# Four small reorderings in an eight-layer transformer kernel on one core: a new order of TensorE's work in the last attention, adapter coefficients moved forward, transposes of the identity at the start, weight sums placed first

## Chip, cores and metric

The kernel runs on one core of a Trainium2 chip. The metric is the time of one execution on the device in microseconds (us). The engines of the core are named as in the profile: PE is TensorE's matmul side and PEld its weight load, DVE is VectorE, ACT is ScalarE, POOL is GpSimd, SP is SyncE, whose queue issues nearly all DMAs. A trailing q (PEq, SPq, DVEq) means the engine's sequencer.

## What is computed

The input is x of shape (2, 512, 512): two batches of 512 tokens of width 512, all in fp32. Eight layers follow each other, each with a layer normalisation in front and the input added to its output. Cut to what matters:

```python
x = x + attn_latent(_layernorm(x))   # 32 heads, keys of 4 latent values, no mask
x = x + ffn_lora(_layernorm(x))      # one matrix plus a rank-16 adapter chosen per batch
x = x + attn_gqa(_layernorm(x))      # 32 query heads in 8 groups of 4, head size 128, rotary, causal
x = x + ffn_lora(_layernorm(x))
x = x + attn_mla(_layernorm(x))      # latent keys and values, causal
x = x + ffn_moe(_layernorm(x))       # top 2 of 8 adapters per token
x = x + attn_mha(_layernorm(x))      # 32 heads of size 16, rotary, causal
x = x + ffn_moe(_layernorm(x))
```

The last attention computes, for each head,

```python
scores = jnp.einsum('bqhd,bkhd->bhqk', q, k) * scale
scores = scores + (1.0 - causal) * MASK_VAL
probs = jax.nn.softmax(scores, axis=-1)
ctx = jnp.einsum('bhqk,bkhd->bqhd', probs, v).reshape(b, s, e)
```

In the adapter layer, `lora_start_indices` say from which batch on which adapter is used. The kernel turns them into one factor per row of the stacked adapter matrices (0 or 1).

## The kernel before

**Memory.** x stays in SBUF as eight tiles of 128 tokens. `xT[b]` is the normalised input of a batch, transposed, in four pieces of 128 channels. PSUM has eight banks of 128 x 512 fp32; `turn()` hands them out in a fixed cycle of eight, so an instruction that takes a bank waits until whatever read the bank eight turns earlier is done. The bank's names in the profile (`sc`, `pj`, `tp`, `av`) say only which of the eight it is.

**Order.** Tile, the layer below the kernel, schedules VectorE, ScalarE, GpSimd and SP by itself, close to the order of the program; each engine then runs its instructions strictly in that order. In the attentions TensorE's order is written out by hand (`manual_schedule`).

**The start.** `Block.__init__` issues the first four loads of x and makes the identity on GpSimd. `attn_latent_small` (first attention) issues its weights and the other four tiles of x on SP, then many small loads. `prepare(0)` normalises the first four tiles (statistics and `xn` on VectorE, one power on GpSimd at L197), transposes each on TensorE (L182), copies it with ScalarE (L187), and multiplies with the latent weights (L156): the first chain gives the keys (L415), the second `cq` (L420), from which the heads follow.

**Adapter layers.** `ffn_lora` runs twice. At its first call (L622 to L638) it loads the start indices and a constant table and computes the factor `k.coef` in eight small VectorE instructions, then scales the adapter matrix `la` with it (L639), multiplies adapters on TensorE (L646, eight outputs), adds the base matrix on VectorE (L650), and multiplies the tokens (L156 chains). The second call finds `k.coef` made.

**Grouped attention.** `attn_gqa` computes the queries of two heads at a time with a Strassen-like scheme: seven half-size products instead of eight, for which `token_sums` (VectorE, L768) and `weight_sums` (GpSimd, L781 to L784, four instructions per pair of heads) prepare sums. The rotary step of a query is two half-height products with the sine on VectorE (L829, L830), then on GpSimd the product with the cosine (L831) and the sum (L832). Scores (L229) need the result. At the start the order written down is latents, keys, token sums, the first pair's weight sums, its queries, the second pair's weight sums, values.

**Last attention.** For each batch, 32 heads are done in eight quartets of four heads. The four heads of a quartet sit in four groups of 32 partitions, so their products can run side by side in the array. A quartet takes on TensorE:
- 16 `score` products S (L1460), one for each of four query tiles and four heads, 128, 256, 384 or 512 columns wide because of the causal mask. VectorE adds the mask and takes the maximum of each row (L1470, and a second instruction that reads the result).
- `maxima`, M: four transposes of these maxima (L1484), then VectorE adds them to the queries (`qm`, L1486), so that the next products come out with the maximum already subtracted.
- 16 `transposed` products T (L1496), keys by queries, 512, 384, 256 or 128 columns wide; ScalarE takes the exponential of each (L1506). After the fourth of a key tile GpSimd masks its diagonal (L1510).
- `values`, V: 64 products with the values into one bank (L1521), copied by ScalarE (L1529).
- `divide`, D: four transposes of the sums (L1535), reciprocal and multiplication on VectorE (L1538, L1539).

`run_quartets` interleaves, at step u, the scores of quartet u+1 with the transposed products of quartet u, one to one; the first four scores and the first four transposed products stand in two blocks. After the first block of each step comes D of quartet u-1; at the end of the step V of quartet u, and then M of quartet u+1. The program has two versions of this attention under a branch, causal by leaving out and causal by adding a mask; the first ran in the profile.

Of the kernel before, what the change touches and what calls it, by code (L numbers as in the profile page):

```python
# [31 lines left out]
F32 = mybir.dt.float32  # L32
I32 = mybir.dt.int32
AF = mybir.ActivationFunctionType
ALU = mybir.AluOpType
AX = mybir.AxisListType

B, S, D = 2, 512, 512
P = 128
NT = S // P  # L40
# [5 lines left out]
class Block:  # L46


    def __init__(self, ctx, tc, x, out):
        nc = self.nc = tc.nc  # L50
        self.tc = tc
        self.out = out
        pool = lambda name, bufs, **kw: ctx.enter_context(tc.tile_pool(name=name, bufs=bufs, **kw))
        self.const = pool("const", 1)
        self.w = pool("w", 2)
        self.work = pool("work", 2)
        self.small = pool("small", 6)
        self.psum = pool("psum", 2, space=bass.MemoryType.PSUM)
        self.turns = 0
        self.held = None  # L60
        self.coef = None

        self.x = [
            self.const.tile([P, D], F32, tag=f"x{t}", name=f"x{t}") for t in range(NTILES)
        ]
        self.source = x
        self.load_x(0)


        self.room = self.const.tile([P, 4 * KC * S], F32, tag="room", name="room")  # L70
        parts = self.room.rearrange("p (n c s) -> p n c s", n=4, c=KC)
        self.xT = [parts[:, b] for b in range(B)]
        self.spare = [parts[:, 2 + i] for i in range(2)]
        self.spare_turn = 0
        self.ident = self.const.tile([P, P], F32, tag="ident", name="ident")
        make_identity(nc, self.ident)
        self.mhalf = self.const.tile([P, 1], F32, tag="mhalf", name="mhalf")
        nc.gpsimd.memset(self.mhalf, -0.5)
        self.ones = self.const.tile([P, 1], F32, tag="ones", name="ones")
        nc.gpsimd.memset(self.ones, 1.0)  # L80

    def load_x(self, b):
        for t in range(b * NT, b * NT + NT):
# [245 lines left out]
    def run_quartets(n, score, maxima, transposed, values, after, extra=()):  # L329
# [5 lines left out]
        for u in range(-1, n + 1):  # L335
# [24 lines left out]
            if u + 1 < n:  # L360
                maxima(u + 1)


def attn_latent_small(k, a):

# [6 lines left out]
    nc, tc = k.nc, k.tc  # L372
    with ExitStack() as ctx:
        lp = ctx.enter_context(tc.tile_pool(name="a", bufs=2))
# [18 lines left out]
        for i in range(2):  # L393
            m = one([P, NT, P], f"nm{i}")
# [81 lines left out]
        for piece in prepare(0):  # L476
            piece()
        k.masks()
        extra = prepare(1) + [fold, fold_bias]

        quartets = [(b, half, i) for b in range(B) for half in range(2) for i in range(4)]
# [123 lines left out]
            k.run_quartets(len(quartets), score, maxima, transposed, values, after, extra)  # L605


def ffn_lora(k, a):

    nc, tc = k.nc, k.tc
    R = 48
    with ExitStack() as ctx:
        lp = ctx.enter_context(tc.tile_pool(name="f0", bufs=2))
        w = k.load(a["f0_w"], [P, KC, D], "w8", 5)

        la = k.load(a["f0_a"], [P, D], "w3", 6)
        lb = k.load(a["f0_b"], [P, D], "w3", 6)  # L620
        bias = k.load_row(a["f0_bias"], D, "bias")
        if k.coef is None:  # L622
            k.coef = k.const.tile([P, 1], F32, tag="coef", name="coef")
            starts = k.load_row(a["f0_starts"], 4, "f0_starts", dtype=I32)
            rows = k.load(a["c_lora"], [P, 4], "c_lora", 1)
            startf = lp.tile([P, 4], F32, tag="startf", name="startf")
            nc.vector.tensor_copy(startf, starts)


            c = lp.tile([P, 4], F32, tag="le", name="le")  # L630
            nc.vector.tensor_scalar(c, startf, rows[:, 3:4], None, ALU.is_le)
            r = lp.tile([P, 3], F32, tag="rank", name="rank")
            both = lp.tile([P, 2], F32, tag="both", name="both")
            nc.vector.tensor_tensor(both, c[:, 1:3], c[:, 2:4], ALU.mult)
            nc.vector.tensor_tensor(r[:, 0:2], c[:, 1:3], both, ALU.subtract)
            nc.vector.tensor_copy(r[:, 2:3], both[:, 1:2])
            nc.vector.tensor_tensor(r, r, rows[:, 0:3], ALU.mult)
            nc.vector.tensor_reduce(k.coef, r, AX.X, ALU.add)  # L638
        nc.vector.tensor_scalar(la, la, k.coef, None, ALU.mult)  # L639

        adapted = [k.w.tile([P, KC, D], F32, tag="w8", name="adapted", bufs=5) for b in range(B)]
        for m in range(KC):
            out = [k.turn() for b in range(B)]
            for b in range(B):
                own = slice(64 * b, 64 * b + R)
                nc.tensor.matmul(  # L646
                    out[b], la[own, bass.ts(m, P)], lb[own], start=True, stop=True
                )
            for b in range(B):
                nc.vector.tensor_tensor(adapted[b][:, m], out[b], w[:, m], ALU.add)  # L650

        for t in range(NT):
            k.add_bias(t, bias)
        for b in range(B):
            for t in range(NT):
                ps = k.turn()
                k.chain(
                    ps, [(k.xT[b][:, c, bass.ts(t, P)], adapted[b][:, c]) for c in range(KC)]
                )
                k.add_to_x(b * NT + t, ps)  # L660
                if b == 0:
                    k.layernorm(NT + t, k.turn, bias=bias)
                else:
                    k.layernorm(t, k.turn, back=True)


def attn_gqa(k, a, bound):
# [7 lines left out]
    nc, tc = k.nc, k.tc  # L675
    G, J = 8, 4
    with ExitStack() as ctx:
# [3 lines left out]
        tables = {}  # L681
# [20 lines left out]
        def latents(b, m):  # L702
            if m == 0:
                ckvT[b] = one([P, KC, S], "ckvT")
            ps = k.turn()
            k.chain(ps, [(wdk[:, c, bass.ts(m, P)], k.xT[b][:, c]) for c in range(KC)])
            nc.scalar.copy(ckvT[b][:, m], ps)
# [85 lines left out]
        def queries(m, i, part):  # L793

            b = groups[m][1]
            a11, a12, diff, a22, both, less, last = ws[m, i]
            x = lambda c, n: tokens(b, c, n)
            add = lambda out, ps, sb: nc.vector.tensor_tensor(out, ps, sb, ALU.add)  # L798
            copies = ends[0][:, :S]
            if part == 0:  # L800
                ps = k.turn()
                product(ps[:, first], a11, x(0, 0))
                product(ps[:, second], both, xs[0])
                nc.scalar.copy(copies, ps)
            elif part == 1:
                q0, q1 = qs[m, 2 * i], qs[m, 2 * i + 1] = [
                    lp.tile([P, S], F32, tag="q", name="q", bufs=3) for r in range(2)
                ]
                ps = k.turn()
                product(ps[:, first], less, xs[1])  # L810
                product(ps[:, second], diff, xs[2])
                add(q0[:, second], ps[:, first], copies[:, first])
                add(q1[:, first], ps[:, second], q0[:, second])
                for out, of in ((q0[:, second], q0[:, second]), (q1[:, second], q1[:, first])):
                    nc.gpsimd.tensor_tensor(out, of, copies[:, second], ALU.add)
            else:
                pair = q0, q1 = qs[m, 2 * i], qs[m, 2 * i + 1]
                ps = k.turn()
                product(ps[:, first], a12, x(1, 0))
                product(ps[:, second], a22, xs[3])  # L820
                add(q0[:, first], ps[:, first], copies[:, first])
                add(q1[:, first], ps[:, second], q1[:, first])
                ps = k.turn()
                product(ps[:, first], last, x(1, 1))
                add(q0[:, second], ps[:, first], q0[:, second])
                for q in pair:
                    t2 = k.work.tile([P, S], F32, tag="xn", name="t2")
                    sin = tables["sinq"]
                    nc.vector.tensor_tensor(t2[0:64], q[64:128], sin[64:128], ALU.mult)  # L829
                    nc.vector.tensor_tensor(t2[64:128], q[0:64], sin[0:64], ALU.mult)  # L830
                    nc.gpsimd.tensor_tensor(q, q, tables["cosq"], ALU.mult)  # L831
                    nc.gpsimd.tensor_tensor(q, q, t2, ALU.add)  # L832

        def softmax(m, j):
# [67 lines left out]
                wdk = k.load(a["b_wdk"], [P, KC, D], "w8", 5)  # L902

        with tc.manual_schedule(engines={mybir.EngineType.PE}):
            for m in range(KC):
                latents(0, m)
            prepare_keys(0)
            token_sums(0)
            weight_sums(0, 0)
            for part in range(3):  # L910
                queries(0, 0, part)
            weight_sums(0, 1)
            prepare_values(0)
            probs = {}
            for n in range(len(units) + J + 1):
# [448 lines left out]
def attn_mha(k, a, exact, rooms):  # L1364
# [9 lines left out]
    with ExitStack() as ctx:  # L1374
# [64 lines left out]
        def core(b, causal):  # L1439
# [104 lines left out]
                )  # L1544

            with tc.manual_schedule(engines={mybir.EngineType.PE}):
                k.run_quartets(8, score, maxima, transposed, values, [divide])
            ctxT = k.other()
            for c in range(T):
                tp = k.turn()  # L1550
# [195 lines left out]
```

## Time and profile before

| what | us |
|---|---|
| runs shown | 2143.32, 2146.19, 2143.63 (median 2143.63) |
| the profiled execution's own time | 2145.26 |
| span of its profile | 2143.50 |
| last attention, batch 0, first score to last transposed sums | 1805.6 to 1906 |
| the same, batch 1 | 1964.8 to 2066 |

The span is the time from the first to the last instruction of the profiled execution; 1.76 us of its own time lie outside. Positions in the profile are counted from the span's start. In a line of the order of time, the columns are start, duration, engine, line and operation, outputs and inputs with their tile names, the shape, the count of merged instructions, and in brackets how long the engine had been idle in front and what ended that. In a stretch's line of busy times, each engine has its busy time and count, then the clock granted to TensorE (1.00 is full), the share of the DMA engines and GB/s.

An fp32 product shows as two passes of one instruction each. Ends of matmuls are modelled, so a matmul's duration says less than the distance between two starts.

### The profile page before, as it was taken

The page shows a single profiled execution, that of the slowest core. Times are in us where ns is not written, and L with a number is a line of the kernel's source. Part 1 is how long each engine was busy: PE and PEld are TensorE (multiplying, and loading weights), DVE is VectorE, ACT ScalarE, POOL GpSimd, SP SyncE. Part 2 cuts the span into 40 slices and gives each one's busy share as a digit, 9 for nine tenths or more (in the row PEclk, how much of TensorE's full clock was granted, in tenths as well). Part 3 has the DMA queues.
Part 4 walks back from the last instruction along what each step waited for, and adds up shares of the span by engine and source line. Part 5 has one row for each costly group of instructions (what it writes and reads, how often), then busy time and mean ns, then how long its engine had stood idle before and what let it go on. Part 6 is the DMA issues. An engine that isn't in the chain of part 4 may idle for free. (4 is left out here: it accounts for less than half of the span.)

```text
span 2143.5 us, 40021 instructions
## 1 busy us (share of the span) xinstructions
PE 2048.5 (96%) x15500; PEld 1147.2 (54%) x15500; DVE 1349.5 (63%) x3571; ACT 749.0 (35%) x2072; POOL 972.9 (45%) x1243
## 2 busy tenths in 40 slices
PE   6999989899999999999999989999999989999988
PEld 3444435566666666666665444545454544554554
DVE  6578754665575566666765557666666675745745
ACT  2455631222232222222222145454445212532531
POOL 1101023767665557666762256555555544215220
PEclk9999999899999999999999999999999999999999
DMA  2000022222222222222221321010101002002001
GB/s 98 16 1 1 20 89 73 86 70 70 89 70 74 71 83 77 73 89 70 72 75 31 115 60 53 21 53 21 49 22 51 2 30 45 1 2 40 2 2 40
DMA packets 70221, 107.44 MB, mean 50 GB/s; under 512 B 13698, under 2 KB 50690, under 8 KB 63236
## 3 DMA queue, kind: packets, MB, share of 16 engines
q1 hardware_dynamic: 69380, 103.71, 15.7%
q8 instruction: 126, 2.06, 0.4%
q10 hardware_dynamic: 640, 1.05, 0.3%
q14 instruction: 75, 0.61, 0.1%
HBM read 80.61 MB, written 2.10 MB: 39 GB/s over the span
## 5 line engine op out<-in xcount | busy, mean ns | idle before, releaser
L250 ACT ACTIVATE room<-room,nmax 128x128 f32<-128x128 f32 (+3 forms) x384 | 212.1, 554 | 478.5 <-DVE nmax L240 477.4
L261 POOL TENSOR_SCALAR room<-room,invs 128x128 f32<-128x128 f32 (+3 forms) x384 | 197.5, 534 | 144.9 <-DVE invs L258 144.9
L301 PE MATMUL sc<-turned,vals 32*128 32x128 f32 (+7 forms) x1090 | 188.4, 424 | 0.0
L301 PE MATMUL tp<-turned,vals 32*128 32x384 f32 (+7 forms) x720 | 164.4, 412 | 2.1 <-DVE q L798 2.1
L229 PE MATMUL sc<-kT,q 128*32 128x256 f32 (+3 forms) x1496 | 135.8, 398 | 11.4 <-DVE invs L258 7.9
L274 DVE STREAM_TRANSPOSE turned<-room 128x1152 f32<-128x1152 f32 x80 | 109.0, 1363 | 42.8 <-POOL room L261 39.8
L301 PEld LDWEIGHTS sc<-turned,vals 32*128 32x128 f32 (+1 forms) x1090 | 122.5, 171 | 9.2 <-issue 4.4
L301 PE MATMUL pj<-turned,vals 32*128 32x256 f32 (+7 forms) x602 | 126.1, 424 | 1.3 <-DVE turned L274 1.3
L831 POOL TENSOR_TENSOR q<-q,cosq 128x512 f32<-128x512 f32 x64 | 95.4, 1491 | 60.0 <-DVE t L830 60.0
L197 POOL TENSOR_TENSOR rstd<-ve,mhalf 128x1 f32<-128x1 f32 x80 | 44.3, 557 | 168.5 <-DVE ve L195 141.3
L229 PE MATMUL tp<-kT,q 128*32 128x32 f32 (+15 forms) x1072 | 98.6, 401 | 11.2 <-DVE invs L258 7.1
L301 PEld LDWEIGHTS tp<-turned,vals 32*128 32x128 f32 (+1 forms) x720 | 97.0, 168 | 14.6 <-issue 6.9
L229 PE MATMUL pj<-kT,q 128*32 128x96 f32 (+15 forms) x1048 | 100.5, 417 | 2.9 <-POOL q L1096 1.9
L156 PE MATMUL sc<-w,room 128*128 128x512 f32 (+1 forms) x224 | 100.5, 595 | 0.0
L301 PE MATMUL av<-turned,vals 32*128 32x384 f32 (+7 forms) x372 | 99.9, 419 | 0.0
L156 PE MATMUL sc<-w,ctxT 128*128 128x512 f32 x208 | 94.2, 595 | 0.0
L250 ACT ACTIVATE probs<-probs,nmax 128x128 f32<-128x128 f32 (+3 forms) x128 | 71.1, 556 | 65.6 <-DVE nmax L240 64.3
L261 POOL TENSOR_SCALAR probs<-probs,invs 128x128 f32<-128x128 f32 (+3 forms) x128 | 65.6, 532 | 60.6 <-DVE invs L258 56.7
L832 POOL TENSOR_TENSOR q<-q,t 128x512 f32<-128x512 f32 x64 | 87.5, 1367 | 4.3
L1093 POOL TENSOR_TENSOR t<-t,sinq 128x512 f32<-128x512 f32 x32 | 40.9, 1277 | 106.1 <-DVE invs L258 101.3
L273 DVE STREAM_TRANSPOSE turned<-room 128x128 f32<-128x128 f32 x80 | 24.4, 305 | 101.0 <-POOL room L261 100.9
L519 PE MATMUL sc<-qm,keys 32*128 32x512 f32 x198 | 85.5, 637 | 0.0
(610 smaller groups left out, 6276.2 us busy)
## 6 DMA issues: line engine op xcount, KB each, us to landing
w<-in_b_wq SPq DMA_DIRECT2D x16, 1024.0 KB, 4.8
w<-in_b_wo SPq DMA_DIRECT2D x16, 1024.0 KB, 5.4
vals<-v SPq DMA_DIRECT2D x256, 64.0 KB, 2.0
w<-in_m_wo SPq DMA_DIRECT2D x8, 1024.0 KB, 6.1
w<-in_b_wk SPq DMA_DIRECT2D x16, 256.0 KB, 2.5
w<-in_b_wupv SPq DMA_DIRECT2D x16, 256.0 KB, 2.6
w<-in_f_w SPq DMA_DIRECT2D x4, 1024.0 KB, 5.5
w<-in_m_wqn SPq DMA_DIRECT2D x8, 384.0 KB, 3.1
```

The costliest lines, as they stand in the source:

```text
L156: last = self.nc.tensor.matmul(out, lhsT, rhs, start=(i == 0), stop=(i == len(pairs) - 1))
L197: self.nc.gpsimd.tensor_tensor(r, ve, self.mhalf, ALU.pow)
L229: nc.tensor.matmul(ps[32 * i : 32 * i + 32, a - lo : b - lo], q[:, at : at + 32], keys[:, a:b], start=True, stop=True,)
L250: nc.scalar.activation(row, row, AF.Exp, bias=nmax, scale=-1.0, accum_out=total[:, qt : qt + 1])
L261: self.nc.gpsimd.tensor_scalar(row, row, inv[:, qt : qt + 1], 1.0, ALU.mult, ALU.mult)
L273: self.nc.vector.transpose(out[:, self.WIDE - P :], probs[:, last : last + P])
L274: self.nc.vector.transpose(out[:, :last], probs[:, :last])
L301: self.nc.tensor.matmul(out[:, :, :n], values(i, j), rhs, start=(j == blocks[0]), stop=(j == stop[i]),)
L519: nc.tensor.matmul(ps, keys[b][rows[g], bass.ts(kc, P)], qm[u][rows[g]], start=True, stop=True)
L831: nc.gpsimd.tensor_tensor(q, q, tables["cosq"], ALU.mult)
L832: nc.gpsimd.tensor_tensor(q, q, t2, ALU.add)
L1093: nc.gpsimd.tensor_tensor(t2, t2, sinq, ALU.mult)
```

## The change

Four edits, with no change to what is computed:

1. After the identity is made, `warm` puts 56 transposes of the identity on TensorE, into a bank that nobody reads.
2. The adapter factor is computed by a function of its own, called in the first attention right after the masks, with its small tiles in another pool. Its two loads are issued on SP's queue ahead of the adapter matrices. In the built program the scaling of the first adapter matrix follows the factor on VectorE, so it too stands in the start of the kernel.
3. In the grouped attention the weight sums of the first two pairs of heads, and the token sums, stand ahead in the program's order; and for the first group (m = 0) the product of the query with the cosine goes to VectorE instead of GpSimd.
4. In the last attention `run_ordered` replaces `run_quartets`. A string gives TensorE's order within a quartet: S the next score, T the next transposed product, M the maxima of the next quartet, | the division of the one before; V follows at the end. Scores run ahead by eight: in a step the last eight scores of quartet u+1 are followed by the first eight of u+2.

```diff
@@ Block.__init__ @@
         make_identity(nc, self.ident)
+        self.warm()
...
+    def warm(self):
+        ps = self.tr()
+        for i in range(56):
+            self.nc.tensor.transpose(ps[:, bass.ts(i % 4, P)], self.ident, self.ident)
...
+    @staticmethod
+    def run_ordered(n, lead, order, score, maxima, transposed, values, after):
+        scores = iter([(u, j, g) for u in range(n) for j in range(NT) for g in (0, 2, 1, 3)])
+        for i in range(lead):
+            score(*next(scores))
+        for u in range(-1, n):
+            left = [(j, g) for j in range(NT) for g in (1, 3, 0, 2)] if u >= 0 else []
+            for step in order:
+                if step == "S":
+                    at = next(scores, None)
+                    if at:
+                        score(*at)
+                elif step == "T" and left:
+                    transposed(u, *left.pop(0))
+                elif step == "M" and u + 1 < n:
+                    maxima(u + 1)
+                elif step == "|" and u > 0:
+                    after(u - 1)
+            if u >= 0:
+                values(u)
+        after(n - 1)
...
@@ attn_latent_small @@
         k.masks()
+        adapter_coefficients(k, a)
         extra = prepare(1) + [fold, fold_bias]
...
+def adapter_coefficients(k, a):
+    nc = k.nc
+    k.coef = k.const.tile([P, 1], F32, tag="coef", name="coef")
+    starts = k.load_row(a["f0_starts"], 4, "f0_starts", dtype=I32)
+    rows = k.load(a["c_lora"], [P, 4], "c_lora", 1)
+    startf = k.sm(4, "startf", 1)
+    nc.vector.tensor_copy(startf, starts)
+    c = k.sm(4, "le", 1)
+    nc.vector.tensor_scalar(c, startf, rows[:, 3:4], None, ALU.is_le)
+    r = k.sm(3, "rank", 1)
+    both = k.sm(2, "adapter", 1)
+    nc.vector.tensor_tensor(both, c[:, 1:3], c[:, 2:4], ALU.mult)
+    nc.vector.tensor_tensor(r[:, 0:2], c[:, 1:3], both, ALU.subtract)
+    nc.vector.tensor_copy(r[:, 2:3], both[:, 1:2])
+    nc.vector.tensor_tensor(r, r, rows[:, 0:3], ALU.mult)
+    nc.vector.tensor_reduce(k.coef, r, AX.X, ALU.add)
...
@@ ffn_lora: the same lines under "if k.coef is None" are gone @@
...
@@ attn_gqa, queries @@
-                    nc.gpsimd.tensor_tensor(q, q, tables["cosq"], ALU.mult)
+                    mul = nc.gpsimd if m else nc.vector
+                    mul.tensor_tensor(q, q, tables["cosq"], ALU.mult)
...
@@ attn_gqa, the first steps @@
+            weight_sums(0, 0)
+            weight_sums(0, 1)
             for m in range(KC):
                 latents(0, m)
+            token_sums(0)
             prepare_keys(0)
-            token_sums(0)
-            weight_sums(0, 0)
             for part in range(3):
                 queries(0, 0, part)
-            weight_sums(0, 1)
             prepare_values(0)
...
@@ attn_mha, core @@
-                k.run_quartets(8, score, maxima, transposed, values, [divide])
+                order = "STTSTSSTSTTSTSTSTTTTS|TTSTMTSSSSSS"
+                k.run_ordered(8, 8, order, score, maxima, transposed, values, divide)
```

## The prediction, as put on record

> **What bounds the kernel now.** I read the page's busy shares first, then the busy time by stage, then the order of time in the four places that the diff touches.
>
> ```profile
> PE 2048.5 (96%) x15500; PEld 1147.2 (54%) x15500; DVE 1349.5 (63%) x3571; ACT 749.0 (35%) x2072; POOL 972.9 (45%) x1243
> ```
>
> TensorE looks full, but its ends are modelled, and what a change brings is read stage by stage. In the last attention a quartet repeats every 11.49 us. The columns are: stretch, length, busy PE, PEld, DVE, ACT, POOL, clock, DMA.
>
> ```profile
> 2009.41:2020.90 11.49, 11.14 (x106) 6.39 (x106) 8.73 (x35) 6.49 (x17) 2.54 (x4) 1.00 0.01 2
> ```
>
> VectorE is the engine with most real work, 8.73 us of 11.49. Its 2.76 us of idle lie in front of three instructions (order of time, same quartet):
>
> ```profile
> 2007.05 1.07 PE L1521 MATMUL pj<-room,vs 128*32 128x512 f32 x8
> ...
> 2009.34 0.66 PE L1484 MATMUL tp<-ident,nm 128*128 128x128 f32 x4
> ...
> 2010.04 0.69 DVE L1486 TENSOR_TENSOR qm<-tp,qs 128x512 f32<-128x512 f32 x1 [1.50 <-PE tp L1484]
> ...
> 2011.85 0.66 PE L1535 MATMUL sc<-ident,raw 128*128 128x128 f32 x4
> ...
> 2012.55 0.26 DVE L1538 RECIPROCAL inv_all<-sc 128x16 f32<-128x16 f32 x1 [0.81 <-PE sc L1535]
> ...
> 2014.85 0.43 DVE L1470 CUSTOM_DVE_ANT_0 tp<-tp,mask 128x256 f32<-128x256 f32 x1 [0.42 <-PE tp L1460]
> ```
>
> The value products (L1521) take TensorE from 2007.05 to 2009.34, 2.29 us. VectorE has only three reductions left to do then, and waits 1.50 us for the transposed maxima behind them, later 0.81 us for the transposed sums.
>
> At the first lora layer TensorE waits for the scaled adapter:
>
> ```profile
> 304.95 0.12 DVE L638 TENSOR_REDUCE coef<-rank 128x1 f32<-128x3 f32 x1
> ...
> 305.60 0.85 DVE L639 TENSOR_SCALAR w<-w,coef 128x512 f32<-128x512 f32 x1
> ...
> 306.50 0.94 PE L646 MATMUL sc<-w,w 48*128 48x512 f32 x1 [4.65 <-DVE w L639]
> ...
> 311.83 3.70 PE L156 MATMUL sc<-adapted,room 128*128 128x512 f32 x8
> ```
>
> At the start of the grouped attention the first scores wait for the rotated query, which stands behind a weight sum on GpSimd:
>
> ```profile
> 367.64 0.73 POOL L781 TENSOR_TENSOR wq_sum<-w 128x256 f32<-128x256 f32 x1
> ...
> 371.84 1.71 POOL L831 TENSOR_TENSOR q<-q,cosq 128x512 f32<-128x512 f32 x1
> ...
> 374.94 0.36 PE L229 MATMUL sc<-kT,q 128*32 128x32 f32 x5 [2.08 <-POOL q L832]
> ```
>
> And the first products of the program run at half speed: eight passes of the first chain take 5.54 us, of the next 3.60 us:
>
> ```profile
> 16.36 5.54 PE L156 MATMUL tp<-room,w 128*128 128x512 f32 x8 [0.68 <-ACT room L187]
> ...
> 21.74 3.60 PE L156 MATMUL sc<-room,w 128*128 128x512 f32 x8
> ```
>
> **What the Trainium skill says.** (1) "TensorE: Matmul & The Clock Gate", Part 1: the array starts at half clock and gets the full one after a busy window of about 3.4 us, losing it after an idle one. The trace agrees: the passes from 16.36 start 0.86 us apart until 19.94, 3.6 us later, then 0.43 us. (2) The same page, Part 4, says a transpose does not count as busy in the same way. The trace does not settle it: at 11.89 to 15.7 sixteen transposes with gaps did not raise the clock. (3) "GPSIMD Engine Reference", 3.1: an fp32 tensor_tensor costs GpSimd about twice VectorE's time. Here L831 takes 1491 ns on GpSimd, the like on VectorE 0.69 us (L768), 1.12 beside a busy GpSimd (L830). (4) "DMA: Bandwidth & Descriptors", Two DMAs through the same engine are not ordered: descriptors of a queue start in order. So a small load waits behind a large one, as the trace shows:
>
> ```profile
> f_starts<-in_f_starts SPq DMA_DIRECT2D x1, 2.0 KB, 6.2
> ```
>
> **Part 1, the string.** The work of a quartet stays the same (16 scores S, 16 transposed products T, values V, maxima M, the division's transposes D); the order is S9 T T S10 T S11 S12 T, S13 T T S14 T S15 T S16, four T, S1' D T T S2' T M T, S3' to S8', V, where S' belong to the quartet after next. The eight banks go round: an instruction waits for the reader of the one eight places before. V stands eight behind M, so **V waits for VectorE's add of M (qm)**; everything on TensorE is queued behind V. The built program bears this out (M and V carry one bank's name) and gives VectorE's order: S9 to S16, S1', D, S2', M, S3' to S8'.
>
> I walk one period, 0 being V's end. Prices: VectorE's start-to-start for 128, 256, 384 and 512 columns is 0.25, 0.38, 0.52, 0.65 us (at 2007.10 and 2007.75 the 512s). A 256-column score issued at 2014.12 reaches VectorE at 2014.85 (0.73); four 512 ones issued at 2010.78 reach ScalarE at 2012.00 (1.22); 384 in between, 0.95.
> - S9 reaches VectorE at 0.95. S9 to S12 4 x 0.52, S13 to S16 4 x 0.65: end 5.63. Their data is in time: S13 needs S9's bank (1.7) and arrives at 2.9, VectorE being ready at 3.0; S16 arrives at 4.4, ready 5.0.
> - S1' to 5.88. D's transposes need S15's bank, 5.2, plus 0.70 (2011.85 to 2012.55): 5.9. Reciprocal and multiply 0.70: 6.6. S2': 6.85.
> - M's transposes need S16's maximum (5.8) and follow T T S' T: start 6.2, at VectorE 6.9; the add 0.69 ends 7.6. V starts 7.7, ends 7.7 + 2.29 = **10.0**.
> - Beside V, VectorE does S3' to S8': 2 x 0.25 + 4 x 0.38 = 2.0 us, then idles until 10.95.
>
> ScalarE needs 6.49 us and GpSimd 2.54, both hidden; the last mask on GpSimd (0.64) has the first 1.9 us of V before its tile is read. So 11.49 falls to 10.0, 1.5 us each. What is late next is qm, then V. Quartets 1 to 6 of a batch: 6 x 1.5 = 9.0. Quartet 7 has no scores beside it and now no M in front: it saves M and the add, 2055.32 to 2056.76, 1.4. Quartet 0: none, since VectorE must first do S3' to S8', and the clock is halved there (passes of 1.22 us at 1815.28) in either order. 10.4 per batch, two batches: **-20.8**. Bounds: -35 (VectorE never waits: 2.76 x 12 + 2.8) and -9 (0.5 a quartet and quartet 7).
>
> **Part 2, coefficients.** Eight small VectorE instructions and the scaling (0.85) move from 302.5 to 306.4 to the first 20 us. Their two loads pass f_a and f_b on SP's queue: issued about 11.95 and 12.4, landing an estimated 17.3 (behind 1 MB of wo, before f_a's 18.45). VectorE stands at the cast until then; queued behind it are only the second batch's normalisations, needed after 30 us, and the scaling waits for f_a, now about 19, ending 20: before keys (21.94) are due. If f_a came 2 us later, keys would slip, not cq: nothing. At the layer: the four products end at 301.84, and the adapter products can follow at once, at full clock (they were 1.7 us a pair when restarted cold, 0.86 warm): 301.85 to 305.4. VectorE then does eight sums of 0.60 with 2.5 us of statistics between from 302.5: the seventh at 309.2. The first chain ends 0.9 later, 310.1, instead of 315.37: **-5.2**; I take -5.0 (bounds -3.5, -5.5). From there to 361 TensorE never pauses over 0.7 us, so it carries. cosq to wq on SP waited for this pool too (305.25), and come about 3 us earlier.
>
> **Part 3, grouped attention.** Only POOL's interleaving with two bias additions changes by "weight sums first": both sums already stood at 315.91 to 321.8, with wq landing first; nothing. The four q*cos move: the first goes to VectorE behind three t products, 371.3 to 372.4 at the contended 1.12, GpSimd adds t by 373.7 instead of 374.9: -1.2. The third the same way, against a 4 us wait at 391.2: -0.3. **-1.5** (bounds 0, -3).
>
> **Part 4, idle transposes.** 56 from 2.0 us. A group of four takes 1.11 cold and 0.66 warm: 0.21 and 0.13 each. If they wake the clock in two windows they end at about 11.5, before the first input at 11.89; the first chain is then 3.6 instead of 5.54 (-1.9), the last group before it 0.45 shorter, and VectorE's new order (L452's 0.69 ahead of the third xn) costs 0.55: -1.8. If the clock falls again in the sparse 11.9 to 16.4: +0.1. If they don't count: 56 x 0.21 end at 13.8, the four groups finish at 17.4 and the chain starts 1.8 late: +1.8. I take **-0.5**.
>
> **Sum.** -20.8 - 5.0 - 1.5 - 0.5 = -27.8. The profiled execution took 2145.26 us (span 2143.50 and 1.76 around it): 2117.5. The median shown, 2143.63, is 1.6 lower: **2115.8**.
>
> **Rivals.** (a) *One wait returns.* D or M comes 0.75 us late each quartet because S16 or T6 waits for ScalarE's bank: period 10.75, 0.75 x 12 + 2.8 = 11.8, total -19: 2125. For it: S13 has only 0.1 us to spare. (b) *VectorE never waits*: -35, total -42: 2102. Against it: V behind qm. (c) *Slower: the clock falls in each quartet.* TensorE now stands from about 6.9 to 7.7 for qm. Cold, V is 4.6, D and M 1.1 each, S9 1.9: a period of about 14.3, +2.8 x 12 = +34, total about +27: 2171. It decides if the streaming share of a window falls as at 294 to 297:
>
> ```profile
> 294.00:296.00 2.00, 0.66 (x4) 0.42 (x4) 0.30 (x1) 0.19 (x1) 0.61 (x1) 1.00 0.00 0
> 296.00:298.00 2.00, 1.55 (x2) 0.75 (x3) 0.00 (x0) 0.40 (x1) 0.00 (x0) 0.64 0.00 0
> ```
>
> There a third busy sufficed; here some 8 of 10 us stream, so it is unlikely. (d) That the string does nothing is excluded by the built order.
>
> **Chances.** Forecast 0.70 (2109 to 2121), (a) 0.20 (2121 to 2129), (b) 0.06, (c) 0.04. The range 2107 to 2128 leaves out (b), (c) and the edge of (a). A measurement here tells about 0.2% (4.3 us) from no change: faster 0.94, same 0.02, slower 0.04.
>
> **What would show it.** A quartet of 10.0 us, VectorE idle only once, some 1.2 us before the first 384 reduction; V released by qm; L646 right behind L588 near 302; the first scores about 1.2 us closer to their query; the first chain at 3.6 us. A period above 10.7, or L646 waiting still, would make me wrong.

## The result, and the profile after

| | median | runs | ratio to before (95% interval) |
|---|---|---|---|
| before | 2144.7 us | 2143.32 to 2146.19 | 1 |
| after | 2120.96 us | 2119.38 to 2125.91 | 0.9893 (0.9875 to 0.9911) |

The change saves 23.7 us; the forecast was 27.8. The profiled execution of after is the slowest of its four, 2125.91 us (span 2124.2, 19.3 less than the span of before); the other three took 2119.4 to 2121.1. Part of what follows explains that difference too.

The busy shares hardly move, so the stages have to be read. First the page's busy line of after, then the busy times of one quartet of its last attention.

```profile
PE 2046.3 (96%) x15556; PEld 1154.9 (54%) x15556; DVE 1349.7 (64%) x3575; ACT 744.9 (35%) x2072; POOL 967.1 (46%) x1239
```

```profile
2007.67:2017.79 10.12, 10.11 (x108) 6.15 (x110) 8.54 (x35) 6.18 (x17) 2.54 (x4) 1.00 0.01 2
```

A quartet takes 10.12 us where it took 11.49, with the same 35 VectorE instructions. The same quartet in order of time:

```profile
2008.61 0.57 DVE L1512 CUSTOM_DVE_ANT_0 pj<-pj,mask 128x384 f32<-128x384 f32 x1 [1.46 <-PE pj L1502]
...
2012.77 0.66 PE L1577 MATMUL sc<-ident,raw 128*128 128x128 f32 x4
...
2013.48 0.25 DVE L1580 RECIPROCAL inv_all<-sc 128x16 f32<-128x16 f32 x1
...
2013.85 0.66 PE L1526 MATMUL sc<-ident,nm 128*128 128x128 f32 x4
...
2014.54 0.69 DVE L1528 TENSOR_TENSOR qm<-sc,qs 128x512 f32<-128x512 f32 x1
...
2015.38 1.06 PE L1563 MATMUL sc<-room,vs 128*32 128x512 f32 x8
...
2017.67 0.58 PE L1502 MATMUL pj<-ks,qs 32*128 32x384 f32 x1
```

VectorE waits once, 1.46 us before the first 384-column reduction; the two waits for M and for D, which were 1.50 and 0.81, are gone (less than 0.1 us is left in front of each). V (L1563) starts 0.15 us after the add of qm has ended.

At the first adapter layer the scaled adapter is no longer waited for; the products (L686) stand right behind the last base product (L624), at full clock, and the transposes behind the first chain (L190) start at 310.48, where they started at 315.37:

```profile
301.54 1.02 PE L624 MATMUL tp<-folded,ctxT 128*128 128x512 f32 x2
302.49 0.69 PE L686 MATMUL sc<-w,w 48*128 48x512 f32 x1
...
310.48 0.60 PE L190 MATMUL pj<-ident,xn 128*128 128x128 f32 x4
```

At the grouped attention the first scores wait 1.46 us for their query, where they waited 2.08. GpSimd's sum in front of them, which took 1.26 us before, takes 1.76 (the first line is of before):

```profile
373.63 1.26 POOL L832 TENSOR_TENSOR q<-q,t 128x512 f32<-128x512 f32 x1
```

```profile
367.62 1.76 POOL L874 TENSOR_TENSOR q<-q,t 128x512 f32<-128x512 f32 x1 [0.63 <-DVE q L873]
369.43 0.32 PE L237 MATMUL sc<-kT,q 128*32 128x32 f32 x5 [1.46 <-POOL q L874]
```

At the start the transposes (L88) run, but the third and fourth input tile come late, and the first chain is as slow as before:

```profile
1.92 8.88 PE L88 MATMUL tp<-ident 128*128 128x128 f32 x56 [1.92 <-POOL ident masks.py:199]
11.81 0.66 PE L190 MATMUL pj<-ident,xn 128*128 128x128 f32 x4 [1.01 <-DVE xn L179]
12.31 0.62 PE L190 MATMUL tp<-ident,xn 128*128 128x128 f32 x4
14.49 1.11 PE L190 MATMUL sc<-ident,xn 128*128 128x128 f32 x4 [1.56 <-DVE xn L179]
15.40 1.06 PE L190 MATMUL pj<-ident,xn 128*128 128x128 f32 x4
17.13 5.53 PE L164 MATMUL tp<-room,w 128*128 128x512 f32 x8 [0.68 <-ACT room L195]
```

To find where the time went I matched the instructions of VectorE, ScalarE and GpSimd in the two traces one by one, and noted how much earlier or later each starts. The shift changes in six stretches only (us, good to about 0.2, all against the profiled execution of before; the experiments below are in the same table):

| kernel | start, to the first heads | to the end of the first adapter layer | start of the grouped attention | start of the latent attention | its four units | last attention |
|---|---|---|---|---|---|---|
| after | +0.8 | -5.7 | -3.3 | +5.4 | +3.5 | -20.0 |
| string alone | -1.0 | -0.1 | 0.0 | 0.0 | +0.1 | -20.4 |
| coefficients alone | +0.3 | -5.7 | -1.5 | 0.0 | -0.1 | 0.0 |
| grouped attention alone | +0.1 | +0.5 | -5.7 | +1.1 | +0.6 | -1.4 |
| transposes alone | -2.3 | +0.5 | +0.1 | 0.0 | +4.1 | -0.1 |
| all without transposes | -2.0 | -5.5 | -4.3 | 0.0 | +0.2 | -19.9 |
| the same, other string | -1.9 | -4.6 | -3.1 | +5.4 | -0.2 | -12.9 |
| all, 128 transposes | +6.4 | -5.5 | -3.3 | +5.4 | -0.2 | -19.8 |

Two stretches of after lose time where the diff touches nothing: 5.4 us at the start of the latent attention (the layer called `attn_mla` in the reference) and 3.5 us in its four units of heads. In the first, the clock is down in after (the ninth figure of the row is the clock):

```profile
1248.00:1252.00 4.00, 3.73 (x8) 1.21 (x6) 1.23 (x10) 0.92 (x5) 0.84 (x2) 0.50 0.07 16
1252.00:1256.00 4.00, 4.00 (x5) 1.02 (x5) 0.00 (x0) 1.66 (x5) 0.00 (x0) 0.50 0.21 49
```

In the second, the clock is full, and TensorE pauses in the midst of small value products, waiting for nothing that the profile shows ("issue"); here the first of the pauses, and all that the view of waits lists of this kind for the whole program (idle in all, how often, median; none in before). It leaves out a fourth, at 1647.65, with 0.13 us of idle:

```profile
1314.43 0.27 PE L309 MATMUL tp<-room,vals 32*64 32x128 f32 x1
1315.23 0.32 PE L309 MATMUL av<-room,vals 32*64 32x128 f32 x1 [0.53 <-issue]
```

```profile
PE tp L309 <- issue: 1.0, 2, 0.5
PE av L309 <- issue: 0.5, 1, 0.5
```

The experiments therefore had two questions: is the string's gain what the prediction said it is, and which part of the change brings the pauses and the fall of the clock.

### The profile page after: what moved, and what is told of

It reads as the page before. It is cut to its first block, busy times and chain, and to the rows that moved or that the text cites. A ratio compares the mean times of both kernels' runs of the same rounds, so it can differ in the third digit from the quotient of the medians.

```text
span 2124.2 us, 40108 instructions
## 1 busy us (share of the span) xinstructions
PE 2046.3 (96%) x15556; PEld 1154.9 (54%) x15556; DVE 1349.7 (64%) x3575; ACT 744.9 (35%) x2072; POOL 967.1 (46%) x1239
## 5 line engine op out<-in xcount | busy, mean ns | idle before, releaser
L873 POOL TENSOR_TENSOR q<-q,cosq 128x512 f32<-128x512 f32 x60 | 89.4, 1491 | 60.6 <-DVE t L870 60.6
L309 PEld LDWEIGHTS tp<-turned,vals 32*128 32x128 f32 (+1 forms) x720 | 96.6, 168 | 15.6 <-issue 8.3
```

Of the source, the lines that this page charges most:

```text
L309: self.nc.tensor.matmul(out[:, :, :n], values(i, j), rhs, start=(j == blocks[0]), stop=(j == stop[i]),)
L873: mul.tensor_tensor(q, q, tables["cosq"], ALU.mult)
```

## Experiments

**One part at a time.** Four kernels, each the kernel before with one part of the diff, as printed above.

The string alone:

> The kernel before with TensorE's order in the last attention as a string, and nothing else of the change. My theory (VectorE's chain from the first 384-column reduction to qm, and then V, sets the period): quartets of 10.1 us where they took 11.5, about -20.3 us in the last attention, as in the changed kernel's trace, so about 2124 us against 2144.7 before. Rival (the four pauses of TensorE that the changed kernel has in the latent attention, +1 us each, come with the string or with chance): the same -20.3, but the latent attention is 3 to 4 us longer, about 2128.

Measured: 2123.54 us against 2145.38 (0.9901, 0.9885 to 0.9916), -21.8. The last attention gives -20.4, and there are no pauses in the latent attention: the string's gain is its own, and the pauses are not the string's.

The coefficients alone:

> The kernel before with the adapter coefficients computed beside the first attention, nothing else. My theory: the base products of the first adapter layer follow the first attention without a pause, the first chain ends about 5.6 us earlier (the stage alone gave -5.65 in the changed kernel), and it carries to the end: about 2139 us. Rival (the coefficients in the first attention's VectorE queue delay the start, so that +0.76 of the changed kernel's late start is theirs): -4.9, and the first chain of the program starts at 17.1 instead of 16.4. Second rival (the gain is lost again at the start of the grouped attention, whose queries wait for loads or GpSimd at a fixed time): within 2 us of before.

Measured: 2138.51 us (0.9964, 0.9951 to 0.9978), -6.9. The adapter layer gives -5.7; the start is not later for it beyond the scatter of the input's arrival (+0.3). A further 1.5 comes at the start of the grouped attention, which this part does not touch.

The grouped attention alone, with both of its edits together:

> The kernel before with the first q*cos of each pair on VectorE, and weight sums and token sums named earlier in the grouped attention, nothing else. Stage times of the two traces say -0.6 at the first scores and a further -1.9 at the third: about -2.5, so 2142. Rival (that gain in the changed kernel came from the layer's earlier loads after the coefficients, not from the q*cos): -0.3 to -1, not to be told from before by its time, and the third scores of the trace as late behind their query as before (4.1 us).

Measured: 2138.28 us (0.9969, 0.9957 to 0.9981), -7.1, far more than any theory gave. The waits behind the query move as in after (2.08 to 1.47 us at the first scores, 4.12 to 3.89 at the third), 0.85 in all. The rest is clock. In before TensorE runs at half clock here from 423 to 430; in this kernel's trace it does not fall there:

```profile
424.00:428.00 4.00, 3.95 (x21) 3.58 (x25) 3.91 (x7) 0.49 (x2) 3.92 (x5) 0.50 0.54 225
```

```profile
424.00:428.00 4.00, 4.00 (x64) 3.73 (x61) 3.92 (x8) 0.45 (x2) 3.92 (x3) 1.00 0.47 190
```

(before, then this kernel; the second figure is TensorE's busy time, the ninth the clock.) With one minus the clock added up in 4-us stretches from 372 to 432, before loses 6.8 us, the coefficients alone 5.1, this kernel 1.7, all without transposes 3.4, after 5.2. The differences to before, with the 0.85 where the edit is in, are -1.7, -6.0, -4.3 and -2.5, against -1.5, -5.7, -4.3 and -3.3 in the table. So the clock accounts for the difference in these traces. It is not an accident of the profiled execution: all six of this kernel (2136.95 to 2142.04 us) are below all 21 runs of before made beside them (2143.60 to 2147.42). Why this edit keeps the clock up, and which half of it, no run shows.

The transposes alone:

> The kernel before with the 56 idle transposes at its start, nothing else. My theory: they wake TensorE's clock, but the built order puts the weight diagonal (0.69 us on VectorE) ahead of the third and fourth normalised tile, TensorE stands 1.6 us, the clock falls again and the first chain starts 0.8 late; and, being 112 more instructions of TensorE, they move the places where its instruction supply has a seam into dense stretches of the latent attention, four pauses of about 1 us: together +3 to +5, about 2149. Rival (the four pauses are chance, or another part's): +0.8, 2145.5, no pause of TensorE ahead of small value products in the latent attention. Rival of the prediction (waking pays): -1.8, 2143.

Measured: 2149.38 us (1.0019, 1.0011 to 1.0026), +4.0: slower. The pauses are there, +4.1 over the four units. In this execution the first chain ran at full clock and the start is 2.3 us earlier, although the same 1.56 us of waiting stand behind the second tile:

```profile
11.88 0.62 PE L190 MATMUL tp<-ident,xn 128*128 128x128 f32 x4
14.06 0.66 PE L190 MATMUL sc<-ident,xn 128*128 128x128 f32 x4 [1.56 <-DVE xn L179]
14.56 0.62 PE L190 MATMUL pj<-ident,xn 128*128 128x128 f32 x4
15.88 3.70 PE L164 MATMUL tp<-room,w 128*128 128x512 f32 x8 [0.71 <-ACT room L195]
```

The clock lived through that gap here and not in after. So the early start is had in some executions. That it is owed to the transposes is not shown: two kernels without them, below, start 2.0 and 1.9 us earlier. The loss in the latent attention was there in all four traces with 56 transposes.

**Without them.** The changed kernel less the call:

```diff
-        self.warm()
```

> The changed kernel without the 56 idle transposes. My theory (112 instructions more on TensorE move a seam of its instruction supply into the value products of the latent attention, in each of its four 110-us units): the pauses before small value products are gone and that attention is 3.5 to 4 us shorter, while the start gains 0.8 at most; together about 2116 to 2117, against 2121 for the changed kernel. Rival (the pauses come from loads that the coefficients let start earlier, or from chance): they stay, and the time is 2120 to 2121. Rival of the prediction (the transposes pay by waking the clock): slower than the changed kernel by 1 to 2 us, 2122 to 2123.

Measured: 2116.82 us against 2144.78 (0.9879, 0.9864 to 0.9894), the fastest kernel of this study. No pause; a unit of the latent attention takes 110.08 us as in before, with the same count of products and loads, against 111.25 in after. After, then this kernel:

```profile
1427.02:1538.27 111.25, 107.66 (x1153) 55.50 (x1153) 72.03 (x213) 54.16 (x165) 63.27 (x88) 1.00 0.11 36
```

```profile
1416.76:1526.84 110.08, 107.04 (x1153) 55.34 (x1152) 71.93 (x213) 54.22 (x165) 63.22 (x88) 1.00 0.11 36
```

Its first chain took 3.70 us, at full clock, with no transposes but the sixteen of its input before it:

```profile
16.20 3.70 PE L156 MATMUL tp<-room,w 128*128 128x512 f32 x8 [0.67 <-ACT room L187]
```

**More of them.** The Trainium skill, "Runtime: NRT & Kernel Launch", Instruction fetch mechanics, says that an engine's instructions are fetched in blocks of 256, a boundary being mostly hidden. That would make a seam (a place where the supply of instructions changes over from one block to the next) that depends on how many instructions stand ahead of it, and 128 transposes, whose 256 instructions are one block, would put it back.

```diff
-        for i in range(56):
+        for i in range(128):
```

> The changed kernel with 128 idle transposes in place of 56: 256 instructions of TensorE (a weight load and a product each) instead of 112. In the trace a unit of the latent attention is about 1152 products and 1152 weight loads long, 2304 instructions, nine times 256, and the pause comes in the same place of each of the four units. My theory (a seam every 256 instructions): with 256 more, the seams fall where they fell before, and the four pauses are gone, though more instructions were added; the units take 110.0 us again, not 110.9. Rival (a pause in any shifted program, or one that grows with what is added): TensorE pauses before small value products stay in all four units. For both, the transposes end near 20 us instead of 10.8 and the first chain starts 4 to 6 us later than the changed kernel's 17.13; total 2121 to 2124 with my theory, 2125 to 2128 with the rival.

Measured: 2128.16 us, one run, above what either theory gave; the start is 6.4 later than in before, 5.6 later than in after, and the clock falls at the start of the latent attention (+5.4). But the pauses are gone, in all four units, and each takes 110.08 us again:

```profile
1431.12:1541.20 110.08, 107.04 (x1153) 55.35 (x1152) 72.07 (x213) 54.24 (x165) 63.22 (x88) 1.00 0.11 36
```

So not the amount of what is added counts but where it puts the rest: 0 and 256 instructions more give no pause, 112 give four. Both kernels with transposes take one bank for them, so a shift in the cycle of banks is not the cause.

The distance of the pauses settles more. Counted in TensorE's records (products, weight loads and the queue's semaphore instructions), they stand exactly 2304 apart, nine times 256, in all four traces with 56 transposes. A unit has 2320, so the pause is not in the same place of each: of the 464 instructions of one dense group of value products, it comes after 419, 403, 387 and 371 in after. Moved back by 112 or on by 144, a seam of that series falls after at most 276 of the 464 or outside them, and there no trace shows a pause. Why only a seam late in the group costs time is not shown. All this agrees with the page's 256; a shorter period that divides 256 but not 112 is not excluded. Where the page has the crossing mostly hidden, the four cost 0.7 to 1.2 us each here, amid products that start every 0.01 to 0.1 us.

**The string's chain.** Two kernels put nearly the same extra VectorE work in two places of the changed kernel's quartet. One writes the add of qm twice:

```diff
                 nc.vector.tensor_tensor(t, tp, q[:, u], ALU.add)
+                nc.vector.tensor_tensor(t, tp, q[:, u], ALU.add)
```

> The changed kernel with the add that makes qm written twice, one behind the other (0.61 us more of VectorE a quartet, between M and V). My theory (V waits for qm, and V's end starts the next quartet's reductions): all of it lands on the period, 10.12 becomes 10.7 to 10.75 us, some 8 to 9 us over the two batches. Rival (the period is set elsewhere, by TensorE's row groups or ScalarE, with VectorE's 1.5 us of idle to absorb it): 10.1 to 10.2.

The other adds two idle additions behind S7' and S8':

```diff
+                if (qt, g) in ((1, 1), (1, 3)):
+                    nc.vector.tensor_tensor(idle, ps[:, :kv], mask[:, lo : lo + kv], ALU.add)
```

> The changed kernel with two idle additions of 256 columns on VectorE (some 0.35 us each, 0.7 together, so a little more work than the other run adds) behind S7' and S8', where VectorE works beside V. My theory (VectorE stands 1.5 us there, waiting for the first 384-column score): nothing, the period stays 10.1 to 10.2 us. Rival (VectorE's total work sets the period, wherever it stands): 10.7 to 10.85.

Measured: periods of 10.93 and 10.12 us (one run each, 2134.49 and 2119.72 in all). The first shows the add, and a reduction of the next quartet that slipped between its two halves, on the path, 0.61 + 0.20 = 0.81 us, and V released by the second add:

```profile
2010.29 0.69 DVE L1528 TENSOR_TENSOR qm<-sc,qs 128x512 f32<-128x512 f32 x1
2010.90 0.29 DVE L1512 CUSTOM_DVE_ANT_0 tp<-tp,mask 128x128 f32<-128x128 f32 x1
...
2011.11 0.69 DVE L1529 TENSOR_TENSOR qm<-sc,qs 128x512 f32<-128x512 f32 x1
...
2011.94 1.06 PE L1564 MATMUL sc<-room,vs 128*32 128x512 f32 x8 [0.82 <-DVE qm L1529]
...
2015.28 0.57 DVE L1512 CUSTOM_DVE_ANT_0 pj<-pj,mask 128x384 f32<-128x384 f32 x1 [1.70 <-PE pj L1502]
```

In the second, the two additions take 0.42 us each, VectorE's wait of 1.46 us shrinks to 0.71, and the period stays:

```profile
2011.65 0.42 DVE L1525 TENSOR_TENSOR idle<-tp,mask 128x256 f32<-128x256 f32 x1
2012.79 0.57 DVE L1514 CUSTOM_DVE_ANT_0 pj<-pj,mask 128x384 f32<-128x384 f32 x1 [0.71 <-PE av L1504]
```

VectorE's chain from the first 384-column reduction to qm, and V behind it, set the period; its total work does not.

**Another string.** The kernel without transposes, with V's bank no longer behind M:

```diff
-                order = "STTSTSSTSTTSTSTSTTTTS|TTSTMTSSSSSS"
-                k.run_ordered(8, 8, order, score, maxima, transposed, values, divide)
+                order = "STSTSTSTSTSTSTSTTTTSTTTTST|SSSMSSS"
+                k.run_ordered(8, 7, order, score, maxima, transposed, values, divide)
```

> As the one without the transposes, and with another string, in which the division stands behind all transposed products and the maxima behind the third score after it, so that the bank that the value products take is no longer behind the maxima; seven scores ahead instead of eight. My theory (what sets the 10.1 us of a quartet is VectorE's chain S9 to qm, and then V): the add of qm runs beside V, and the durations of the changed kernel's quartet give 9.5 us, so 0.6 in 12 quartets and a little at the last ones, 7 to 9 us less: about 2108. Rival (something else than V's wait for qm is as late, ScalarE's exponentials or the full row groups): a period of 10.0 to 10.2 as before, about 2116. Second rival (D or M now comes late, the division's reading of VectorE is in front of the first reductions): a period above 10.2, 2118 or more.

Measured: 2126.88 us (0.9905, 0.989 to 0.992); a period of 10.55. My theory of this string fails, and so does the rival of 10.1; it went the second rival's way:

```profile
2011.64 0.74 DVE L1504 CUSTOM_DVE_ANT_0 sc<-sc,mask 128x512 f32<-128x512 f32 x1
...
2012.48 0.18 PEld L1530 LDWEIGHTS sc<-qm,ks 32*128 32x128 f32 x1 [0.35 <-DVE nm L1504]
...
2013.13 0.66 PE L1569 MATMUL tp<-ident,raw 128*128 128x128 f32 x4
...
2014.14 0.66 PE L1518 MATMUL sc<-ident,nm 128*128 128x128 f32 x4
...
2015.37 1.07 PE L1555 MATMUL tp<-room,vs 128*32 128x512 f32 x8
```

The fourteenth transposed product (L1530 at 2012.48) stands eight banks behind S15 and waits for its reduction (the DVE line). In TensorE's order the last transposed products, S1', the division's transposes (D, L1569), three scores, M (L1518), three scores and V follow it. From D to V alone that is 2.2 us, one after the other. Freeing V of one bank left a longer row in front of it, behind another wait.

**The fall of the clock at the latent attention.** The kernel without transposes and the same with the other string are one program up to the last attention. One shows the fall and one does not:

```profile
1236.50:1256.50 20.00, 15.94 (x113) 8.21 (x113) 9.43 (x47) 9.87 (x38) 7.43 (x12) 1.00 0.15 35
```

```profile
1238.50:1258.50 20.00, 18.17 (x53) 8.58 (x53) 6.23 (x35) 6.21 (x28) 5.84 (x11) 0.58 0.14 33
```

So these 5.4 us belong to the execution, not to the code. The five runs of the kernel with the other string show it too: two took 2120.4 and 2120.9 us at a mean clock of 0.986, three 2126.9 to 2128.5 at 0.980 or 0.981. Its median thus holds the fall: it lies 10 us above that of the first string, while the last attention is only 7 us longer in the table. The 5.4 us are also about what sets the profiled execution of after above the other three.

## Why the prediction was right, point by point

- **Part 1, the string: right.** The walk gave S9 at VectorE at 0.95, D at 5.9, qm's end at 7.6, V at 7.7, a period of 10.0; counted from V's end at 2007.55 the trace has 1.06, 5.93, 7.7, 7.83 and 10.12. VectorE's one wait was put at 1.2 us and is 1.46. The sum of -20.8 came out as -20.0 in after and -20.4 alone. That V is released by qm is what the two kernels with extra work show. Of the rivals, one wait returning (10.75) and VectorE never waiting did not happen, and in the steady quartets the clock stayed at 1.00, so rival (c) did not happen either.
- **Part 2, coefficients: right, a little small.** -5.0 was taken, -5.7 measured in after and alone. The cast waited for its load until 17.81 (estimate 17.3) and the scaling ended at 20.3 (estimate 20), ahead of keys at 22.70: the cover named for it held.
- **Part 3, grouped attention: the mechanism was right, its size not.** The first scores were to come 1.2 us closer to their query and the third 0.3; it was 0.62 and 0.23. At the first scores VectorE's product ended when the prediction said, and the term that was too small is GpSimd's sum behind it: it was put at about the 1.26 us of before and took 1.76, beside a VectorE that was still making the products of the second head. The stretch still gave -3.3, since less of it ran at half clock, a term that the step left out. The same falls explain why the parts don't add up: coefficients alone and this part alone gain 1.5 and 5.7 here, together 3.3 or 4.3. The four medians sum to -31.8 and the whole is -23.7; some 3 to 4 us of the difference are this overlap, the rest is not settled.
- **Part 4, idle transposes: this step failed.** "I take -0.5", with bounds of -1.8 and +1.8, was +4.0 alone, and about +4.1 between the medians of the kernels with and without them. Of its three cases the traces show two, by execution: woken and kept (-2.3 against before, transposes alone) and fallen again (+0.8, after); since kernels without the transposes also started up to 2.0 us earlier, the -2.3 is not shown to be their gain. What no bound held is that 112 instructions shift TensorE's stream, and that this costs 3.5 to 4.1 us a millisecond later. Rightly named was the diagonal of weights ahead of the third tile: it starts at 13.28 in after, and TensorE stands 1.56 us.

The forecast of 2115.8 is nearly the time of the kernel without the transposes (2116.82), and what after lacks to it is about that step. But this closeness is in part luck: in the traces the grouped attention gave 1.8 us (after) and 2.8 us (without transposes) more than forecast, through a clock that the prediction did not reckon with there, and the start of the kernel without transposes gave 2.0 us with none of the transposes that were to bring them.

## What to carry to other kernels

Find the one wait that the engine's order makes, walk a period from it with durations of the profile, and prove the chain by putting work into it and beside it: an add of 0.6 us cost 0.8 in one place, and 0.8 us of idle additions cost nothing in the other. A few instructions added at the start of a long unrolled program can cost time far away, so compare the traces also where the diff touches nothing. Where TensorE's clock falls, compare several executions before giving an edit the credit or the blame.

## What the hardware showed beyond that

- Transposes do wake the clock. The Trainium skill, "TensorE: Matmul & The Clock Gate", Part 4, says that they don't count as busy in the same way. Here the 56 went from 10 to 21 transposes per 2 us without anything else on TensorE, about 3 us after the first of them in one execution (transposes alone) and about 5 in another (after), and the groups behind them took 0.66 where cold ones take 1.11. Even the sixteen of the input, 11.7 to 15.6, were enough in two executions without the 56 (a first chain of 3.70 us) and not enough in four others (5.4 to 6.2).
- A gap of 1.56 us behind the same instructions of TensorE lost the clock in two executions (after, the add written twice) and not in two others (transposes alone, the idle additions).
